# Two filters per product and one 1024-column add in the mixing stage of a spectral convolution

## Chip, cores and metric

The kernel runs on one core of a Trainium2 chip. The metric is the device time of one execution in microseconds. Names of engines: PE is the TensorE matmul unit (PEld its weight load), DVE is VectorE, ACT is ScalarE, POOL is GpSimd, SP is SyncE, which here issues DMAs. All data is 32-bit float.

## What is computed

Two layers run one after the other on a tensor of 4 images, 128 channels, 128 x 128 pixels. The first is a state-space (Mamba) layer over windows of 8 x 8 pixels. The second is a convolution in the frequency domain followed by a small network per pixel. The change lies in the second layer, in the lines that multiply by Phi and Theta (W1, gelu and W2 follow):

```
Xf = jnp.fft.rfft2(z, axes=(-2, -1))
Phi = Phi_f_real + 1j * Phi_f_imag
Uf = Xf[:, :, None, :, :] * jnp.conj(Phi)[None, None]
U = jnp.fft.irfft2(Uf, s=(gx, gy), axes=(-2, -1))
S = jnp.einsum('bdlxy,lhd->bhxy', U, Theta)
...
H = jax.nn.gelu(H, approximate=False)
out = jnp.einsum('bhxy,dh->bdxy', H, W2) + b2[None, :, None, None]
```

There are 16 filters (the index l). For each, Theta[l] mixes 128 channels into 128, and Phi[l] is a complex factor for each frequency. Since both are linear, the kernel does the mixing before the inverse transform: for each frequency row y (65 of them, the half spectrum) it forms the sum over l of conj(Phi[l]) times (Theta[l] times Xf).

## The kernel before

Four stages follow each other: the state-space layer (`mamba_layer`, about two thirds of the time), the forward transform (`spectra`), the mixing (`mix`), and the inverse transform with the network (`images_and_mlp`). Only `mix` is touched. Its instructions stand in the order in which the Python code calls them, on each engine by itself; engines wait for each other through semaphores that the framework sets where tiles are written, read and reused.

`mix` goes over the 65 rows y, and within a row over the 16 filters k. For one row the input is `o.xk`: 128 channels by 4 images (B) by real and imaginary part (r) by 128 frequencies in x. The steps of one filter:

- `products` (lines 657 to 665) has PE multiply: for each r and each image, one product of 128 x 128 with `theta[:, k]`, 128 columns. In 32-bit float each product is two matmul records in the profile, each with its weight load. [...] `products` returns four terms, each a tile, the part r of the result that it goes to, and which of three factor tables (real, imaginary, negated imaginary) it is scaled by.
- `mine` (lines 681 to 690) has DVE take each of the four terms from PSUM, scale it by the factor and add it to the accumulator `acc` of its row: one operation of 512 columns each.
- `ahead` (lines 667 to 679) does the same for the row after, on ACT and POOL: ACT scales the term from PSUM into a tile `part` in SBUF, and POOL adds `part` to `acc` (the first filter is written to `acc` by ACT without an add).

`APART` on line 642 names the filters that go to ACT and POOL: 0, 2, 5, 7, 10 and 12. The other ten go to DVE. While DVE adds its ten filters of row y, ACT and POOL gather their six of row y+1; the accumulator (3 buffers) then passes to DVE, whose first operation of a row therefore depends on POOL's last add for that row. PE does the products of both in the order of the loop on lines 712 to 720; row 0 has no row before it, so there DVE does all 16.

`finish` (lines 692 to 709) writes an accumulator to memory, with 32 DMAs on SP's queue: 2 for image 0, and for the other images 6 with 4 mirrored ones each. It is called for row y-1 in row y after filter 3, and then `load` fetches the input of row y+3 (4 buffers).

Of the kernel before, what the change touches and what calls it, by code (L numbers as in the profile page):

```python
# [13 lines left out]
F32 = mybir.dt.float32  # L14
BF16 = mybir.dt.bfloat16
AF = mybir.ActivationFunctionType
ALU = mybir.AluOpType
PSUM = bass.MemoryType.PSUM

P = 128  # L20
# [8 lines left out]
NL = 16  # L29
# [3 lines left out]
SG = (0, 16, 32, 48, 60, KY)  # L33
# [20 lines left out]

APART = {2: -2, 4: 0, 8: 3, 12: 6, 14: 10, 18: 15, 20: 17, 24: 20}

# [4 lines left out]
HQ = 32  # L61


def mamba_layer(tc, d, x, x1, zb, deltas, dus, results):
# [16 lines left out]
    with ExitStack() as ctx:  # L81
# [91 lines left out]
        def take(slot, f):  # L173
            takes.setdefault(slot, []).append(f)
# [197 lines left out]
        def fetch(s):  # L372

            if 0 <= s < U * R:
                r, k = divmod(s, U)
                u = SimpleNamespace(o=rs[r], r=r, h=k // 16, ch=k // 8 % 2, i=k // 2 % 4, jp=k % 2, apart=k in APART)
                units[s] = u
# [18 lines left out]
        for r in range(R):  # L396
            for k, at in APART.items():
                take(U * r + at - 3, partial(fetch_du, U * r + k))
# [226 lines left out]
def load_row(tc, xf, y, t):  # L625
    for q in range(2):
        tc.nc.sync.dma_start(t[:, :, :, q], xf[y // YG][y % YG, :, :, q])


def mix(tc, theta, phi, sign, xf, firsts, sf, mirrors, first):  # L630

    nc = tc.nc  # L640
    B = len(sf)
    APART = (0, 2, 5, 7, 10, 12)
    with ExitStack() as ctx:
        ctx.enter_context(tc.manual_schedule())
        sb = ctx.enter_context(tc.tile_pool(name="m_sb", bufs=3, reuse_waits="tile"))
        ps = ctx.enter_context(tc.tile_pool(name="m_ps", bufs=4, space=PSUM, reuse_waits="tile"))
        nc.vector.tensor_scalar(phi[0], phi[0], sign, None, ALU.mult)
        nc.vector.tensor_scalar(phi[2], phi[1], -1.0, None, ALU.mult)
        rows = {y: SimpleNamespace(xk=t) for y, t in enumerate(firsts)}

        def load(y):
            if y < KY:
                rows[y] = o = SimpleNamespace()
                o.xk = sb.tile([P, B, 2, 2, W // 2], F32, tag="xk", name="xk", bufs=4)
                load_row(tc, xf, y, o.xk)

        def products(o, k):
            v = []
            for r in range(2):
                t = ps.tile([P, B, P], F32, tag=f"v{r}", name=f"p_v{r}")  # L660
                for b in range(B):
                    nc.tensor.matmul(t[:, b], o.xk[:, b, r], theta[:, k], start=True, stop=True)  # L662
                v.append(t)

            return [(v[of], r, by) for first in range(2) for r, of, by in ((0, first, first), (1, 1 - first, 2 * first))]

        def ahead(y, k):
            if y == KY:
                return
            o = rows[y]  # L670
            if k == APART[0]:
                o.acc = sb.tile([P, B, 2, P], F32, tag="acc", name="acc")
            for i, (v, r, by) in enumerate(products(o, k)):
                into = part = o.acc[:, :, r]
                if k != APART[0] or i >= 2:
                    part = sb.tile([P, B, P], F32, tag="part", name="part", bufs=8)
                nc.scalar.activation(part, v, AF.Copy, scale=phi[by][:, k, y : y + 1])  # L677
                if part is not into:
                    nc.gpsimd.tensor_tensor(into, into, part, ALU.add)  # L679

        def mine(y, k):
            o = rows[y]
            if y + k == 0:
                o.acc = sb.tile([P, B, 2, P], F32, tag="acc", name="acc")
            for i, (v, r, by) in enumerate(products(o, k)):
                into, factor = o.acc[:, :, r], phi[by][:, k, y : y + 1]
                if y + k == 0 and i < 2:
                    nc.vector.tensor_scalar(into, v, factor, None, ALU.mult)
                else:
                    nc.vector.scalar_tensor_tensor(into, v, factor, into, ALU.mult, ALU.add)  # L690

        def finish(y):
            if y >= 0:
                o = rows.pop(y)
                at = y - 1 if 0 < y < KY - 1 else KY - 2 + y // (KY - 1)
                g = int(np.searchsorted(SG, at, "right")) - 1
                for q in range(2):
                    hs = slice(q * (P // 2), (q + 1) * (P // 2))
                    nc.sync.dma_start(sf[0][g][:, q, at - SG[g]], o.acc[:, 0, :, hs])
                if y in [k if k < KY else KY - 1 for k in SG[1:]]:  # L700
                    first(g)
                for b in range(1, B):
                    for r in range(2):
                        part = o.acc[:, b, r].rearrange("p (q h) -> p q h", h=HQ)
                        nc.sync.dma_start(sf[b][:, :, r, at], part)

                        for k in range(4):
                            to, of = (slice(32 * j + (k < 2), 32 * j + 32) for j in (k, k ^ 1))
                            nc.sync.dma_start(mirrors[b][to, :, r, at], part[of])

        load(2)
        for y in range(KY):
            for k in range(NL):
                if k not in APART or y == 0:
                    mine(y, k)
                if k in APART:
                    ahead(y + 1, k)
                if k == 3:
                    finish(y - 1)
                    load(y + 3)  # L720
        finish(KY - 1)


# [118 lines left out]
def conv_kernel(ctx: ExitStack, tc: tile.TileContext, d, out):  # L842
# [16 lines left out]
    with ExitStack() as stages:  # L859
# [43 lines left out]
        def first_image(g):  # L903
            for q in range(2):
                nc.sync.dma_start(spec[q][:, SG[g] : SG[g + 1]], sf[0][g][:, q])

        mix(tc, m.theta, m.phi, m.sign, xf, m.firsts, sf, mirrors, first_image)
    images_and_mlp(tc, c, spec, sp.close, sf, mirrors, x1, out)

# [74 lines left out]
```

## Time and profile before

| | us |
|---|---|
| median of 3 runs | 9695.65 (9645.32 to 9696.60) |
| profiled execution, its own time | 9703.76 |
| its span, first to last instruction | 9702.0 |
| mixing, first product to last DVE operation of L690 | 7060.0 to 8984.5 |

| engine | busy in the whole span | its part in the mixing, instructions | mean ns |
|---|---|---|---|
| PE | 8698.3 (90%) | L662, 16640 | 277 |
| PEld | 4716.0 (49%) | L662, 16640 | 193 |
| DVE | 8582.0 (88%) | L690, 2622 | 743 |
| ACT | 6311.0 (65%) | L677, 1408 and 128 | 688 and 684 |
| POOL | 8053.3 (83%) | L679, 1408 | 1280 |

The shares over the whole span mix four stages with different limits; what a change in `mix` is worth is read from the stretch between 7060 and 8985. Matmuls are pipelined: the 277 ns of one is longer than the distance to the next, so distances are read from counts over a stretch. In a group of the profile, "idle before" is the time in which the engine stood before these instructions, with the engine and line that ended most of it. The granted clock is the share of TensorE's full clock.

### The profile page before, as it was taken

Reading aid. Unit: us, or ns where it says so; the run is one execution under the profiler, and the core shown is the slowest. Engines: PE = TensorE matmul, PEld = TensorE weight load, DVE = VectorE, ACT = ScalarE, POOL = GpSimd, SP = SyncE. Lnnn points to the kernel's source line nnn. Section 1 sums busy time; section 2 is a strip of 40 time slices with the busy share of each in tenths; the row PEclk is TensorE's granted clock in tenths of the full one; section 3 lists DMA queues with packets and bytes.
Section 4 is the critical chain, followed back from the end, with each engine's and each line's share of the span. In section 5 each row is a group of like instructions: output and inputs, shape, how many; then the busy total and the mean of one; then the engine's idle time right before and its main releaser. Section 6 shows DMA issues by size and latency. Waiting matters only on the chain. (4 is left out here: it accounts for less than half of the span.)

```text
span 9702.0 us, 140663 instructions
## 1 busy us (share of the span) xinstructions
PE 8698.3 (90%) x46868; PEld 4716.0 (49%) x46868; DVE 8582.0 (88%) x6989; ACT 6311.0 (65%) x12163; POOL 8053.3 (83%) x3196
## 2 busy tenths in 40 slices
PE   7888888888888888888888888887899999999999
PEld 3333333333333333333333333332899999999665
DVE  6999999999999999999999999998589999999433
ACT  5777777777777777777776777775545555554333
POOL 6999999999999999999999999997389999998120
PEclk8999999999999999999999999998999999999999
DMA  6787777788887787787787777876832323232453
GB/s 180 236 243 236 235 239 236 235 242 237 236 241 233 235 241 231 236 242 237 235 245 230 237 241 237 237 241 191 241 79 52 59 51 58 52 58 52 161 206 130
DMA packets 1504097, 1878.58 MB, mean 194 GB/s; under 512 B 681828, under 2 KB 749684, under 8 KB 1496308
## 3 DMA queue, kind: packets, MB, share of 16 engines
q1 hardware_dynamic: 1502796, 1869.45, 66.3%
q8 instruction: 373, 6.11, 0.3%
q14 instruction: 352, 2.88, 0.1%
q10 hardware_dynamic: 576, 0.14, 0.0%
HBM read 1540.52 MB, written 328.60 MB: 193 GB/s over the span
## 5 line engine op out<-in xcount | busy, mean ns | idle before, releaser
L475 POOL TENSOR_TENSOR hs<-hs,bc 128x2048 f32<-128x2048 f32 x1024 | 4646.9, 4538 | 559.3 <-DVE hs L449 433.0
L449 DVE TENSOR_TENSOR_SCAN hs<-dA,p_du 128x1024 f32<-128x1024 f32 x1536 | 3451.0, 2267 | 0.0
L429 ACT ACTIVATE dA<-dr,A 128x504 f32<-128x504 f32 x3072 | 1996.4, 707 | 9.9 <-DVE hs L449 8.6
L445 DVE TENSOR_TENSOR p_du<-p_du,bc 128x1024 f32<-128x1024 f32 x1536 | 1823.5, 1217 | 174.8 <-PE p_du L414 173.7
L662 PE MATMUL p_v<-theta,xk 128*128 128x128 f32 x16640 | 1881.6, 277 | 46.0 <-ACT part L677 28.1
L690 DVE SCALAR_TENSOR_TENSOR acc<-p_v,phi,acc 128x512 f32<-128x512 f32 x2622 | 1769.7, 743 | 150.3 <-PE p_v L662 124.7
L662 PEld LDWEIGHTS p_v<-theta,xk 128*128 128x128 f32 x16640 | 1876.3, 193 | 51.3 <-ACT part L677 31.9
L679 POOL TENSOR_TENSOR acc<-acc,part 128x512 f32<-128x512 f32 x1408 | 1737.7, 1280 | 140.9 <-ACT part L677 96.0
L414 PE MATMUL p_du<-du,c_rsel 32*128 32x512 f32 x6144 | 1295.6, 655 | 235.8 <-DVE hs L449 232.8
L677 ACT ACTIVATE part<-p_v,phi 128x512 f32<-128x512 f32 x1408 | 884.9, 688 | 547.8 <-PE p_v L662 506.8
L394 POOL TENSOR_TENSOR ur<-ur,bc 128x1024 f32<-128x1024 f32 x512 | 1212.5, 2368 | 16.6 <-DMA ur<-du 16.6
L485 PE MATMUL p_y<-hs,c_ssel 128*32 128x512 f32 x8192 | 1130.1, 624 | 52.4 <-POOL hs L475 52.4
L449 DVE TENSOR_TENSOR_SCAN hs<-p_du,ur 128x1024 f32<-128x1024 f32 x512 | 1165.9, 2277 | 0.0
L242 PE MATMUL p_conv<-tn,W_conv 128*128 128x512 f32 x2016 | 1110.9, 656 | 0.8
L414 PEld LDWEIGHTS p_du<-du,c_rsel 32*128 32x128 f32 x6144 | 358.5, 187 | 896.2 <-issue 525.0
L247 ACT ACTIVATE xc<-p_conv,b_conv 128x512 f32<-128x512 f32 x252 | 173.1, 687 | 884.5 <-PE p_conv L242 884.5
L429 ACT ACTIVATE p_du<-dr,A 128x504 f32<-128x504 f32 x1024 | 701.6, 685 | 33.5 <-DMA dr<-delta 0.2
L208 PE MATMUL ln_back<-ident,cs 128*128 128x128 f32 x2008 | 320.2, 308 | 366.9 <-ACT cs L202 366.9
L242 PEld LDWEIGHTS p_conv<-tn,W_conv 128*128 128x128 f32 x2016 | 340.9, 198 | 528.6 <-issue 310.8
L208 PEld LDWEIGHTS ln_back<-ident,cs 128*128 128x128 f32 x2008 | 268.9, 209 | 586.3 <-ACT cs L202 534.4
L485 PEld LDWEIGHTS p_y<-hs,c_ssel 128*32 128x32 f32 x8192 | 163.1, 109 | 748.2 <-issue 368.9
L257 PE MATMUL p_bc<-xc,c_W_bc 128*128 128x512 f32 x1016 | 498.7, 613 | 0.1
(136 smaller groups left out, 8887.6 us busy)
## 6 DMA issues: line engine op xcount, KB each, us to landing
dr<-delta SPq DMA_DIRECT2D x4096, 256.0 KB
ur<-du SPq DMA_DIRECT2D x1024, 256.0 KB
delta<-dl SPq DMA_DIRECT2D x128, 512.0 KB
du<-du SPq DMA_DIRECT2D x128, 512.0 KB
xf<-x SPq DMA_DIRECT2D x40, 832.0 KB
xk<-xf SPq DMA_DIRECT2D x130, 256.0 KB
xt<-in_x_dram SPq DMA_DIRECT2D x64, 512.0 KB
x<-x1t SPq DMA_DIRECT2D x64, 512.0 KB
```

Source lines behind the costliest of these rows:

```text
L242: nc.tensor.matmul(windows(o.pc), W_conv[:, ch, k], moved, start=(k == 0), stop=(k == K - 1))
L394: nc.gpsimd.tensor_tensor(fetched[s], fetched[s], spread(o.bc[0, h], 2), ALU.mult)
L414: nc.tensor.matmul(u.bank[:, j % 2], c["rsel"][p, u.i], half(u.o.du[p, u.ch], u.h), start=True, stop=True)
L429: nc.scalar.activation(u.dA[:, q, :, 1:], u.delta[:, q].rearrange("p (w t) -> p w t", t=L)[:, :, 1:], AF.Exp, scale=A[:, g : g + 1],)
L445: nc.vector.tensor_tensor(u.bu, u.bu, spread(u.o.bc[0, u.h], 2), ALU.mult)
L449: nc.vector.tensor_tensor_scan(u.hs.rearrange("p q t -> p (q t)"), u.dA.rearrange("p q w t -> p (q w t)"), u.bu.rearrange("p q t -> p (q t)"),
L475: nc.gpsimd.tensor_tensor(hs, hs, spread(u.o.bc[1, u.h], 4), ALU.mult)
L485: nc.tensor.matmul(o.py[h, ch][32 * j : 32 * j + 32], c["ssel"][:, u.i], units[s + j // 2].hs[:, j % 2], start=(u.i == 0), stop=False, ski ...
L662: nc.tensor.matmul(t[:, b], o.xk[:, b, r], theta[:, k], start=True, stop=True)
L677: nc.scalar.activation(part, v, AF.Copy, scale=phi[by][:, k, y : y + 1])
L679: nc.gpsimd.tensor_tensor(into, into, part, ALU.add)
L690: nc.vector.scalar_tensor_tensor(into, v, factor, into, ALU.mult, ALU.add)
```

## The change

Filters are taken in pairs k, k+1. [...] `products` returns four terms, one for each r and each filter of the pair, with the two factors for the real and imaginary result. ACT writes both results of a term into one `part` of 1024 columns (4 buffers in place of 8), and POOL adds it at once. The accumulator's dimensions are reordered to (2, B, 128). The pairs go in a written order, `ORDER`; the pairs that go to ACT and POOL are 0, 6 and 12 (six filters, as before). `finish` and `load` stand behind pair 4.

```diff
-    APART = (0, 2, 5, 7, 10, 12)
+    ORDER = (2, 0, 4, 8, 6, 10, 14, 12)
+    APART = (0, 6, 12)
...
-        ps = ctx.enter_context(tc.tile_pool(name="m_ps", bufs=4, space=PSUM, reuse_waits="tile"))
+        ps = ctx.enter_context(tc.tile_pool(name="m_ps", bufs=2, space=PSUM, reuse_waits="tile"))
...
-                t = ps.tile([P, B, P], F32, tag=f"v{r}", name=f"p_v{r}")
+                t = ps.tile([P, B, 2, P], F32, tag=f"v{r}", name=f"p_v{r}")
                 for b in range(B):
-                    nc.tensor.matmul(t[:, b], o.xk[:, b, r], theta[:, k], start=True, stop=True)
+                    nc.tensor.matmul(t[:, b], o.xk[:, b, r], theta[:, k : k + 2], start=True, stop=True)
                 v.append(t)
-            return [(v[of], r, by) for first in range(2) for r, of, by in ((0, first, first), (1, 1 - first, 2 * first))]
+            return [(v[r][:, :, j], k + j, ((0, 2), (1, 0))[r]) for r in range(2) for j in range(2)]
...
             if k == APART[0]:
-                o.acc = sb.tile([P, B, 2, P], F32, tag="acc", name="acc")
-            for i, (v, r, by) in enumerate(products(o, k)):
-                into = part = o.acc[:, :, r]
-                if k != APART[0] or i >= 2:
-                    part = sb.tile([P, B, P], F32, tag="part", name="part", bufs=8)
-                nc.scalar.activation(part, v, AF.Copy, scale=phi[by][:, k, y : y + 1])
-                if part is not into:
-                    nc.gpsimd.tensor_tensor(into, into, part, ALU.add)
+                o.acc = sb.tile([P, 2, B, P], F32, tag="acc", name="acc")
+            for i, (v, f, by) in enumerate(products(o, k)):
+                part = o.acc
+                if k != APART[0] or i:
+                    part = sb.tile([P, 2, B, P], F32, tag="part", name="part", bufs=4)
+                for r in range(2):
+                    nc.scalar.activation(part[:, r], v, AF.Copy, scale=phi[by[r]][:, f, y : y + 1])
+                if part is not o.acc:
+                    nc.gpsimd.tensor_tensor(o.acc, o.acc, part, ALU.add)
...
-            for i, (v, r, by) in enumerate(products(o, k)):
-                into, factor = o.acc[:, :, r], phi[by][:, k, y : y + 1]
-                if y + k == 0 and i < 2:
-                    nc.vector.tensor_scalar(into, v, factor, None, ALU.mult)
-                else:
-                    nc.vector.scalar_tensor_tensor(into, v, factor, into, ALU.mult, ALU.add)
+            for i, (v, f, by) in enumerate(products(o, k)):
+                for r in range(2):
+                    into, factor = o.acc[:, r], phi[by[r]][:, f, y : y + 1]
+                    if first and i == 0:
+                        nc.vector.tensor_scalar(into, v, factor, None, ALU.mult)
+                    else:
+                        nc.vector.scalar_tensor_tensor(into, v, factor, into, ALU.mult, ALU.add)
...
-            for k in range(NL):
+            for k in ORDER:
                 if k not in APART or y == 0:
                     mine(y, k)
                 if k in APART:
                     ahead(y + 1, k)
-                if k == 3:
+                if k == 4:
                     finish(y - 1)
                     load(y + 3)
```

More of the change, by code (lines that the diff above doesn't have):

```diff
@@ L671, in ahead @@
             if k == APART[0]:
-                o.acc = sb.tile([P, B, 2, P], F32, tag="acc", name="acc")
-            for i, (v, r, by) in enumerate(products(o, k)):
-                into = part = o.acc[:, :, r]
-                if k != APART[0] or i >= 2:
-                    part = sb.tile([P, B, P], F32, tag="part", name="part", bufs=8)
-                nc.scalar.activation(part, v, AF.Copy, scale=phi[by][:, k, y : y + 1])
-                if part is not into:
-                    nc.gpsimd.tensor_tensor(into, into, part, ALU.add)
+                o.acc = sb.tile([P, 2, B, P], F32, tag="acc", name="acc")
[7 more added lines that the diff above has]
+                    nc.gpsimd.tensor_tensor(o.acc, o.acc, part, ALU.add)
         def mine(y, k):
             o = rows[y]
-            if y + k == 0:
-                o.acc = sb.tile([P, B, 2, P], F32, tag="acc", name="acc")
-            for i, (v, r, by) in enumerate(products(o, k)):
-                into, factor = o.acc[:, :, r], phi[by][:, k, y : y + 1]
-                if y + k == 0 and i < 2:
-                    nc.vector.tensor_scalar(into, v, factor, None, ALU.mult)
-                else:
-                    nc.vector.scalar_tensor_tensor(into, v, factor, into, ALU.mult, ALU.add)
+            first = y == 0 and k == ORDER[0]
+            if first:
+                o.acc = sb.tile([P, 2, B, P], F32, tag="acc", name="acc")
+            for i, (v, f, by) in enumerate(products(o, k)):
[5 more added lines that the diff above has]
+                        nc.vector.scalar_tensor_tensor(into, v, factor, into, ALU.mult, ALU.add)
         def finish(y):
@@ L698, in finish @@
                     hs = slice(q * (P // 2), (q + 1) * (P // 2))
-                    nc.sync.dma_start(sf[0][g][:, q, at - SG[g]], o.acc[:, 0, :, hs])
+                    nc.sync.dma_start(sf[0][g][:, q, at - SG[g]], o.acc[:, :, 0, hs])
                 if y in [k if k < KY else KY - 1 for k in SG[1:]]:
@@ L703, in finish @@
                     for r in range(2):
-                        part = o.acc[:, b, r].rearrange("p (q h) -> p q h", h=HQ)
+                        part = o.acc[:, r, b].rearrange("p (q h) -> p q h", h=HQ)
                         nc.sync.dma_start(sf[b][:, :, r, at], part)
```

## The prediction, made before the changed kernel ran

> **What bounds the kernel now.** The page's slices show three parts, and only lines of the mixing function change, so I read the windows of that stage first, then the groups of its lines, then its waits. Columns of the windows: stretch, length, busy time of PE, weight loads, DVE, ACT and POOL with instruction counts, granted clock, DMA.
>
> ```profile
> 7200.00:7400.00 200.00, 196.78 (x1746) 196.40 (x1745) 183.65 (x273) 102.57 (x165) 186.99 (x152) 0.99 0.28 49
> 8600.00:8800.00 200.00, 200.00 (x1792) 199.93 (x1791) 188.96 (x280) 104.55 (x169) 188.68 (x154) 1.00 0.29 52
> ```
>
> PE is full; DVE and POOL are at 94%, ACT at 52%. 1792 matmuls in 200 us are 111.6 ns each. A row has 16 filters x 8 products, and each product is two records (16640 in all for 65 rows), so a row is 256 x 0.1116 = 28.57 us and PE sets it.
>
> ```profile
> L662 PE MATMUL p_v<-theta,xk 128*128 128x128 f32 x16640 | 1881.6, 277 | 46.0 <-ACT part L677 28.1
> L690 DVE SCALAR_TENSOR_TENSOR acc<-p_v,phi,acc 128x512 f32<-128x512 f32 x2622 | 1769.7, 743 | 150.3 <-PE p_v L662 124.7
> L679 POOL TENSOR_TENSOR acc<-acc,part 128x512 f32<-128x512 f32 x1408 | 1737.7, 1280 | 140.9 <-ACT part L677 96.0
> L394 POOL TENSOR_TENSOR ur<-ur,bc 128x1024 f32<-128x1024 f32 x512 | 1212.5, 2368 | 16.6 <-DMA ur<-du 16.6
> ```
>
> DVE waits almost only for PE, never for POOL, though in the built program, before and after, the first DVE instruction of a row carries a wait for POOL: a row's share from POOL must be complete before DVE adds to it. Before, the last POOL filter of a row is 12, and DVE has 13, 14 and 15 (12 operations, 8 us) to do first. From the timeline I take the spacing in a dense stretch (start, length, count):
>
> ```profile
> 7066.69 43.21 DVE L690 SCALAR_TENSOR_TENSOR acc<-p_v,phi,acc 128x512 f32<-128x512 f32 x65 [0.85 <-PE p_v L662]
> 8609.90 25.89 POOL L679 TENSOR_TENSOR acc<-acc,part 128x512 f32<-128x512 f32 x21
> 8619.11 1.84 ACT L677 ACTIVATE part<-p_v,phi 128x512 f32<-128x512 f32 x3 [0.21 <-PE p_v L662]
> 9299.60 1.88 PE L802 MATMUL p_h<-mu,c_W 128*128 128x512 f32 x4
> 9301.32 1.88 PE L811 MATMUL p_o<-g,c_W 128*128 128x512 f32 x4
> ```
>
> DVE: (43.21-0.743)/64 = 0.664 us. POOL: (25.89-1.277)/20 = 1.231, less than the 1.277 of one. ACT: (1.84-0.687)/2 = 0.577, so two are 1.26. A 512-column matmul takes 1.72/4 = 430 ns.
>
> **The change part by part.** The stage runs from 7060.0 to 8984.5, 1924.5 us of the profiled execution's 9703.76.
>
> *Products of 256 columns.* No row here has such a matmul in a stretch: at least half of 430 = 215 ns, at most twice 111.6 = 223. I take 217, the straight line between both rows. A row is then 128 x 0.217 = 27.8 us, 0.8 less than now, at most 50 us over 65 rows. This is the gain if PE stays the bound. A half of a pair (one tile, 8 records) is filled in 1.74 us.
>
> *DVE and ACT* have as many operations as before (40 and 24 a row, 512 columns each). They read PSUM in four runs of 128 instead of one; the same form with four runs on the accumulator runs now at 743 ns, so I add nothing. Bounds: no gain, and 0.3 us each (the strided copy of p_ix, 1.04 us).
>
> *GpSimd* gets 11 adds of 1024 columns for 22 of 512. L394 says 2.37 us. Before, neighbouring adds went to different halves of acc and overlapped by 0.046; now each needs the sum of the one before. I take 2.37 + 0.05 = 2.42; bounds 2.32 (overlap remains) and 2.57 (0.2 for a handoff, as in ACT's 0.21 after PE). A row is 26.6 us, below 28.57, so POOL's total isn't the bound.
>
> *The order of pairs* is the costly part. Call pairs on DVE D and on ACT/POOL A: D2 A0 D4 D8 A6 D10 D14 A12, and A belongs to the next row. A12 now stands last and D2 of the next row first, so the 8 us of cover are gone: DVE stands until POOL has added all four parts of A12. Behind the waiting DVE stand D2's PSUM tile and all products that need DVE's tiles. And PE can't run ahead, because the two buffers of each tile hold two pairs in place of four filters in half the size: slot 0 takes D2, D4, A6, D14; slot 1 A0, D8, D10, A12. PE is in order, so A12 is filled after D10 and D14.
>
> One row from its first DVE operation (T0): D2, D4 and D8 end at 23 x 0.664 + 0.743 = 16.0. This frees the second tile of slot 1; 0.2 later (the 0.21 that PE waited after ACT) PE fills D10's second half, both halves of D14 and the first of A12: 4 x 1.74 = 7.0, so 23.2. To ACT 0.17 (a matmul's 275 ns less its 111.6), two ACT 1.26: 24.6. To POOL 0.06 (a gap in the timeline at 7105.6), four adds 9.68: 34.4, and 0.1 to DVE: the next T0 is at 34.5. Nothing earlier breaks this chain: D4's first half is there at 4.9 (wanted at 5.3), D8's at 9.2 (10.6), D10's at 16.2 (16.0; its 0.2 late is no part of the chain), POOL is through with A6 at 23.5. DVE itself needs 26.6 and stands for 7.6.
>
> *What that does to the clock.* PE ends A0 at 32.4 and can go on with D4 only when DVE has read D2's first tile, 2.9 after T0: 5.1 us idle. Idle gaps of that size are in the state-space stage (last bracket: idle before):
>
> ```profile
> 6642.34 1.13 PE L414 MATMUL p_du<-du,c_rsel 32*128 32x512 f32 x4
> 6652.76 2.08 PE L414 MATMUL p_du<-du,c_rsel 32*128 32x512 f32 x4 [4.05 <-DVE hs L449]
> 6658.35 1.13 PE L414 MATMUL p_du<-du,c_rsel 32*128 32x512 f32 x4
> ```
>
> After 4.05 us the same four matmuls take 2.08 in place of 1.13, until about 5 us later; all gaps over 4 us that I looked at (4.6, 4.7, 6.1, 11.4, 15.4) are followed by 3.5 to 5.6 us of this. So D4's first half takes 3.48, is there at 6.6, and DVE is 1.3 late: 35.7 us a row. The second half ends at 9.2, wanted at 9.25.
>
> [...]
>
> *DMAs.* SP's row of 32 issues takes some 25 us and no new ones are added; finish and load come at the same place behind DVE's last operation, and a longer row gives them more time. The 155 us that ACT waits now for the accumulator's stores go away, off the path.
>
> *Sum.* Row 0 has no such wait at its start: 1.9 to the first tile, 52 DVE operations until D14's first tile is free (34.5), then 0.3 + 1.74 + 0.17 + 1.26 + 0.06 + 9.68 + 0.1 = 13.3; with 2 us of half clock at the start, as now (272 matmuls in 32.4 us instead of 30.4), 52. Then 63 x 35.7 = 2249 and DVE's last row 26.6: 2328, 403 more than 1924.5. On 9703.76 this is 10,107; on the median of the runs, 9695.65, 10,099. I say 10,100.
>
> **The rivals.**
> *PE stays the bound* (faster). If POOL's last add came before DVE is through with D14, the row would be PE's 27.8: -50, 9,646. For it: PE at 100% today and no DVE wait for POOL. It decides from the point where the chain above is 28.57 or less, 5.9 us shorter; all four adds would have to take 0.95 each, against 2.37 in L394. 5%.
> *The wait, with the clock kept up*: 34.5 a row, 52 + 2174 + 27 = 2253, +328, 10,024. For it: gaps of 2.5 and 2.7 us at 6646 and 6690 were followed by 1.13 at first. Against it: the gap here is 5. 20%.
> *The wait with dearer operations*: 0.2 more a POOL add and half clock for 7 us give some 37.2 a row, +500, 10,195; DVE at 0.3 us more each would add 24 x 0.3 = 7 a row and pass 10,500. Against the last: the present accumulator is strided and costs nothing. 10%.
> *A smaller wait* (9,745 to 9,960): PE takes the fills in another way than I see. 4%. *No change* 2%.
>
> **How the numbers follow.** Wait and half clock have 59%, with a time of 10,100. The range: low end from the warm clock with POOL at 2.32 and DVE at 0.655 (34.0 a row, 2220, +296: 9,992) less 47 for the spread of the runs (9645 to 9697); high end from half clock for 7 us (36.9 a row, +478: 10,174) and some 36 of the 54 us that the stage now takes beyond PE's 1857 and the 13 at its end. So 9,945 to 10,210, with about 84% inside: nearly all of the first case and the second rival, half of the third. A change under 0.5% (48 us) can't be told from none here. Faster 4% (the PE rival is -50, just past the bound, with 1 of its 5% inside it), same 3%, slower 93%.
>
> **What would show it.** In the profile after: DVE's first operation of each row idle 7 to 9 us behind POOL's acc, 64 times (some 500 us in all); PE idle about 5 us a row behind DVE, and mean clock in this stage near 0.93; POOL adds at 2.3 to 2.5 us; rows 34 to 37 us apart; PE's 256-column matmuls 215 to 223 ns apart in dense stretches. If DVE waits for PE instead, or POOL's wait is under 2 us, the prediction is wrong. If the wait is there and the clock stays at 1.0, it is the second rival.

## The result: 4.4% slower, and the profile after

| | before | changed |
|---|---|---|
| median us | 9696.12 (9645.32 to 9703.24, 4 runs) | 10115.11 (10089.85 to 10115.90, 4 runs) |
| profiled execution, its own time | 9703.76 | 10115.90 |
| mixing, first product to end of DVE's last | 1924.5 | 2336.2 (7059.8 to 9396.0) |

The ratio is 1.0438, with an interval of 1.0399 to 1.0476. The stage alone is longer by 411.7 us, and the profiled executions differ by 412.1: everything else is as it was.

The groups of the changed kernel that stand for the three shown of before (count, busy time, mean ns, idle time before and its main cause):

```profile
L663 PE MATMUL p_v<-theta,xk 128*128 128x256 f32 x8320 | 1976.9, 401 | 362.5 <-DVE acc L694 346.5
L694 DVE SCALAR_TENSOR_TENSOR acc<-p_v,phi,acc 128x512 f32<-128x512 f32 x2622 | 1743.2, 743 | 587.8 <-POOL acc L681 490.2
L681 POOL TENSOR_TENSOR acc<-acc,part 128x1024 f32<-128x1024 f32 x704 | 1656.7, 2357 | 635.2 <-ACT part L679 595.1
```

All three engines now stand idle: PE 362 us where it had 46, DVE 588 where it had 150, POOL 635 where it had 141. DVE's idle time is put down to POOL, which it did not wait for before. The mean of a DVE operation is still 743 ns.

Two stretches of 200 us (columns as before):

```profile
7200.00:7400.00 200.00, 172.04 (x733) 145.40 (x731) 148.09 (x224) 82.01 (x139) 146.23 (x63) 0.93 0.23 41
8600.00:8800.00 200.00, 169.24 (x712) 142.68 (x712) 145.98 (x220) 81.65 (x138) 148.39 (x64) 0.93 0.23 41
```

PE went from full to 85%, DVE and POOL from 94% to 73%, and the granted clock from 1.0 to 0.93. No engine is the bound; a chain through all four is. The timeline of one row shows it (start, length, idle before):

```profile
8217.40 5.42 PE L663 MATMUL p_v<-theta,xk 128*128 128x256 f32 x24 [0.45 <-DVE acc L694]
...
8224.70 5.36 DVE L694 SCALAR_TENSOR_TENSOR acc<-p_v,phi,acc 128x512 f32<-128x512 f32 x8 [7.44 <-POOL acc L681]
...
8227.57 14.01 PE L663 MATMUL p_v<-theta,xk 128*128 128x256 f32 x56 [4.75 <-DVE acc L694]
...
8231.23 21.16 DVE L694 SCALAR_TENSOR_TENSOR acc<-p_v,phi,acc 128x512 f32<-128x512 f32 x32 [1.17 <-PE p_v L663]
...
8249.24 4.74 ACT L679 ACTIVATE part<-p_v,phi 128x512 f32<-128x512 f32 x8 [6.28 <-PE p_v L663]
8250.65 16.81 POOL L681 TENSOR_TENSOR acc<-acc,part 128x1024 f32<-128x1024 f32 x7 [1.33 <-ACT part L679]
...
8260.33 5.36 DVE L694 SCALAR_TENSOR_TENSOR acc<-p_v,phi,acc 128x512 f32<-128x512 f32 x8 [7.94 <-POOL acc L681]
```

DVE starts a row at 8224.70, after 7.44 us behind POOL. PE had stopped at 8222.8 and goes on 4.75 us later, when DVE has emptied a tile. DVE is through its first pair in 5.36 and then waits 1.17 for the next products. A12 reaches ACT at 8249.24 and POOL at 8250.65; the first four of its seven adds are A12's, and 9.7 us later DVE starts the next row, 35.6 us after the last. Over all rows these starts are 35.8 us apart on average (before: 28.57 us of PE work).

### The profile page after: what moved, and what is told of

Read it like the earlier page. It is cut to its first block, busy times and chain, and to the rows that moved or that the text cites. A ratio compares the mean times of both kernels' runs of the same rounds, so it can differ in the third digit from the quotient of the medians.

```text
span 10113.9 us, 121963 instructions
## 1 busy us (share of the span) xinstructions
PE 8793.8 (87%) x38548; PEld 4505.0 (45%) x38548; DVE 8556.4 (85%) x6989; ACT 6263.9 (62%) x12163; POOL 7974.0 (79%) x2492
## 5 line engine op out<-in xcount | busy, mean ns | idle before, releaser
L663 PE MATMUL p_v<-theta,xk 128*128 128x256 f32 x8320 | 1976.9, 401 | 362.5 <-DVE acc L694 346.5
L694 DVE SCALAR_TENSOR_TENSOR acc<-p_v,phi,acc 128x512 f32<-128x512 f32 x2622 | 1743.2, 743 | 587.8 <-POOL acc L681 490.2
L681 POOL TENSOR_TENSOR acc<-acc,part 128x1024 f32<-128x1024 f32 x704 | 1656.7, 2357 | 635.2 <-ACT part L679 595.1
L663 PEld LDWEIGHTS p_v<-theta,xk 128*128 128x128 f32 x8320 | 1666.1, 202 | 673.1 <-issue 362.3
L679 ACT ACTIVATE part<-p_v,phi 128x512 f32<-128x512 f32 x1408 | 835.7, 705 | 1220.4 <-PE p_v L663 1213.9
```

What stands on the lines that cost most here:

```text
L663: nc.tensor.matmul(t[:, b], o.xk[:, b, r], theta[:, k : k + 2], start=True, stop=True)
L679: nc.scalar.activation(part[:, r], v, AF.Copy, scale=phi[by[r]][:, f, y : y + 1])
L681: nc.gpsimd.tensor_tensor(o.acc, o.acc, part, ALU.add)
```

## The experiments

The order of the pairs, the coarse units, the clock and the wide add are all part of one change. The first four kernels take them apart.

**Another order, nothing else.**

```diff
-    ORDER = (2, 0, 4, 8, 6, 10, 14, 12)
+    ORDER = (0, 2, 6, 4, 8, 12, 10, 14)
```

> The changed kernel with one line altered: the pairs go A0 D2 A6 D4 D8 A12 D10 D14, so that two DVE pairs (16 operations, 10.6 us) follow the last POOL pair of a row. Theory (the row change waits for POOL's sum because A12 stands last): DVE's wait for POOL falls from 490 us to under 30, a row from 35.7 to about 28.7 us, the stage from 2336 to 1885 to 1940 us, the whole to 9,660 to 9,715 us, at or below the kernel before. Rival (the pairs themselves cost: two buffers in place of four, PSUM read in four runs, 1024-column adds): the row stays above 33 us and the whole above 10,000 us.

Measured: 9680.62 us against 9694.30 for the kernel before (ratio 0.9987, 0.9977 to 0.9996). One line gives back the whole loss. DVE's wait for POOL is gone from the list; the stage's waits (engine, who it waited for, us in total, times, longest) are now:

```profile
ACT part L679 <- PE p_v L663: 377.1, 117, 6.2
ACT acc L679 <- DMA mirrors<-acc: 276.7, 34, 15.6
DVE acc L694 <- PE p_v L663: 142.9, 66, 11.3
```

So in this order neither 256-column products nor two buffers nor PSUM read in four runs costs anything near 400 us. In the second line ACT waits for an accumulator whose stores are still under way. The changed kernel has no such wait; the kernel before has it too, but shorter:

```profile
ACT acc L677 <- DMA mirrors<-acc: 155.1, 24, 12.8
```

**The order on single filters.** The kernel before, with its finer tiles, adds and four buffers, in the order of the changed one:

```diff
-    APART = (0, 2, 5, 7, 10, 12)
+    ORDER = (2, 3, 0, 1, 4, 5, 8, 9, 6, 7, 10, 11, 14, 15, 12, 13)
+    APART = (0, 1, 6, 7, 12, 13)
...
-            for k in range(NL):
+            for k in ORDER:
```

> The kernel before, single filters, 128-column products, four buffers, 512-column adds, with only the order of the changed kernel: filters 2 3 0 1 4 5 8 9 6 7 10 11 14 15 12 13, of which 0 1 6 7 12 13 go to ACT and POOL. Theory: the wait belongs to the order, not to the pairs: about 34.8 us a row, DVE idle behind POOL about 7 us a row, whole about 10,040 us. Rival (the coarse tiles cause it): the finer tiles hide the turn, and the time stays within 50 us of 9,696.

Measured, in one run: 9937.02 us, 243 above before. The waits of this kernel hold this line:

```profile
DVE acc L692 <- POOL acc L680: 385.0, 126, 5.9
```

The order alone brings the wait, which settles against the rival, but 100 us less than expected. The 126 waits are two a row: each half of the accumulator has its own last add, and DVE's first operation starts when the first half is ready. I had reckoned with one wait for the whole. So of the 419 us lost, 243 come with the order on single filters too, and the other 176 only where the order meets the coarser units. This run doesn't tell wide tiles from wide adds; narrow adds in the changed kernel, below, give back 108.

This run also shows something of the clock. PE waits 205.8 us for DVE in this kernel, in 69 waits, 3.2 us at the longest, and equal gaps are not all followed by the same clock. Here are the 8 us behind two of them, of 3.21 and 3.22 us:

```profile
8197.08:8205.08 8.00, 8.00 (x71) 8.00 (x72) 8.00 (x13) 0.00 (x0) 5.12 (x5) 1.00 0.21 33
8229.12:8237.12 8.00, 8.00 (x57) 8.00 (x58) 7.70 (x12) 0.00 (x0) 5.10 (x5) 0.79 0.23 35
```

The first stretch has the full clock and 71 matmul records, the second a mean of 0.79 and 57.

**The clock.** The changed kernel with more work for PE: the second tile of pair 0 for ACT is computed three times over, into the same place.

```diff
-                for b in range(B):
+                for b in [*range(B)] * (1 + again * r):
                     nc.tensor.matmul(t[:, b], o.xk[:, b, r], theta[:, k : k + 2], start=True, stop=True)
...
-            for i, (v, f, by) in enumerate(products(o, k)):
+            for i, (v, f, by) in enumerate(products(o, k, 2 * (k == APART[0]))):
```

> The changed kernel with work added: PE makes the second tile of pair 0's products for ACT three times over (16 more matmul records a row, 3.5 us), so that its idle time at the row change falls from 5.0 to about 1.5 us. Theory (after the long gap the next products run at half clock and make DVE 1.3 us late): the clock stays at 1.0, DVE's wait for PE after its first 8 operations goes, a row falls from 35.7 to about 34.6 us, the whole by 70 to 85 us to about 10,035 us, though PE does 6% more. Rival (the half clock is hidden by the wait for POOL, or the clock doesn't follow the gap): 10,115 us or more.

Measured: 10023.81 us, ratio to before 1.0338 (1.0321 to 1.0355); 91 us faster than the changed kernel's 10115.11, with 1024 matmul records more. The group of DVE and a stretch:

```profile
L694 DVE SCALAR_TENSOR_TENSOR acc<-p_v,phi,acc 128x512 f32<-128x512 f32 x2622 | 1738.2, 743 | 505.9 <-POOL acc L681 485.0 <-PE p_v L663 20.8
```

```profile
7200.00:7400.00 200.00, 185.56 (x837) 157.09 (x837) 153.11 (x232) 81.09 (x136) 151.62 (x65) 1.00 0.24 43
```

The clock is back at 1.00, and DVE's idle time behind PE is 20.8 us where the waits of the changed kernel have 96.7:

```profile
DVE acc L694 <- PE p_v L663: 96.7, 101, 3.9
```

The wait for POOL is nearly as long as in the changed kernel, 485 us against 490. The half clock was thus a cost of its own on top of the wait: 91 us in all, 1.4 a row, of which 76 are DVE's wait for PE.

**Narrow adds.** The changed kernel with two adds of 512 columns, each right behind its ACT operation:

```diff
                 for r in range(2):
                     nc.scalar.activation(part[:, r], v, AF.Copy, scale=phi[by[r]][:, f, y : y + 1])
-                if part is not o.acc:
-                    nc.gpsimd.tensor_tensor(o.acc, o.acc, part, ALU.add)
+                    if part is not o.acc:
+                        nc.gpsimd.tensor_tensor(o.acc[:, r], o.acc[:, r], part[:, r], ALU.add)
```

> The changed kernel with each 1024-column add of POOL split into two of 512, one for each half of the accumulator, each behind its own ACT operation. Theory: POOL takes 1.23 us an add and 27.1 us a row against 26.6, but the chain at the row change shortens: the first add starts 0.6 us earlier, and DVE's first operation needs only the half that is ready 1.2 us before the last. About 1.0 us less a row, 65 us in all, 10,050 us. Rival (the larger add saves POOL fixed cost where it counts): 10,115 us or more.

Measured: 10006.68 us (1.0325, 1.0309 to 1.0340), 108 us faster than with the wide add, though POOL is busy longer (1734 us against 1657). The sign was right and the size, 65 us, too small. DVE's waits show both parts:

```profile
L694 DVE SCALAR_TENSOR_TENSOR acc<-p_v,phi,acc 128x512 f32<-128x512 f32 x2622 | 1755.1, 744 | 474.2 <-POOL acc L681 403.7 <-PE p_v L663 66.5
```

The wait for POOL fell by 87 us (490.2 to 403.7), 1.35 a row where I had 1.0, and the wait for PE, which I had left out, by 30 (96.7 to 66.5). One row of it:

```profile
8207.73 0.75 DVE L694 SCALAR_TENSOR_TENSOR acc<-p_v,phi,acc 128x512 f32<-128x512 f32 x1 [5.83 <-POOL acc L681]
8208.95 4.70 DVE L694 SCALAR_TENSOR_TENSOR acc<-p_v,phi,acc 128x512 f32<-128x512 f32 x7 [0.47 <-POOL acc L681]
...
8211.16 24.55 PE L663 MATMUL p_v<-theta,xk 128*128 128x256 f32 x104 [3.70 <-DVE acc L694]
...
8213.81 2.73 DVE L694 SCALAR_TENSOR_TENSOR acc<-p_v,phi,acc 128x512 f32<-128x512 f32 x4 [0.16 <-PE p_v L663]
```

DVE starts on the first half while POOL adds the second. PE's gap shrinks to 3.70 us, and in this row DVE is only 0.16 late after its first pair, against 1.17 in the changed kernel's.

**One pair later.** The changed kernel with A12 one place earlier:

```diff
-    ORDER = (2, 0, 4, 8, 6, 10, 14, 12)
+    ORDER = (2, 0, 4, 8, 6, 10, 12, 14)
```

> The changed kernel with the last two pairs exchanged: D10 A12 D14, so that one DVE pair (8 operations, 5.3 us) follows the last POOL pair. Theory: part of the cover is back, DVE's wait for POOL falls from 7.7 to about 5 us a row, but D14 now waits 1.8 us for PE, because A12 is filled before it: a row about 34.9 us, 60 us less in all, about 10,055 us. Rival (any DVE pair behind A12 hides its sum): 9,750 us or less.

Measured, in one run: 10014.74 us, 100 us less than the changed kernel where I expected 60. One row:

```profile
8207.99 5.36 DVE L694 SCALAR_TENSOR_TENSOR acc<-p_v,phi,acc 128x512 f32<-128x512 f32 x8 [4.54 <-POOL acc L681]
...
8210.86 13.74 PE L663 MATMUL p_v<-theta,xk 128*128 128x256 f32 x56 [4.17 <-DVE acc L694]
...
8214.28 15.89 DVE L694 SCALAR_TENSOR_TENSOR acc<-p_v,phi,acc 128x512 f32<-128x512 f32 x24 [0.93 <-PE p_v L663]
...
8232.24 5.36 DVE L694 SCALAR_TENSOR_TENSOR acc<-p_v,phi,acc 128x512 f32<-128x512 f32 x8 [2.06 <-PE p_v L663]
```

DVE waits 4.54 us for POOL (expected: about 5), 0.93 after its first pair, and 2.06 before D14 (expected: 1.8). So one DVE pair behind the last POOL pair is indeed not cover enough. PE's gap is 4.17 us here.

**Four accumulators.** What was left in the first experiment is the wait for the stores, so the better order and the kernel before each got a fourth buffer, in both lines that allocate it. In the kernel with pairs:

```diff
-                o.acc = sb.tile([P, 2, B, P], F32, tag="acc", name="acc")
+                o.acc = sb.tile([P, 2, B, P], F32, tag="acc", name="acc", bufs=4)
```

> The first experiment (A0 D2 A6 D4 D8 A12 D10 D14) with a fourth accumulator buffer, so that ACT no longer waits for the accumulator's stores (277 us in all there). Theory: PE's idle time in the stage falls from 71 to about 30 us, a row to 28.7 us, the stage to about 1886 us, the whole to 9,645 to 9,675 us, some 30 us below the first experiment. Rival (those waits are ACT's own slack): no change from 9,681.

> The kernel before with a fourth accumulator buffer and nothing else. Theory: it too loses time to the accumulator's stores, and comes to PE's bound, 28.6 us a row, about 1875 us for the stage, the whole to 9,640 to 9,660 us; then the pairs with the better order win nothing over single filters, since what 256 columns save on PE (0.5 us a row) goes into the wait for coarser tiles. Rival (products of 256 columns are worth their 0.5 to 0.8 us a row): this one stays 30 us or more above the run with pairs and four buffers.

Measured: 9648.12 with pairs (0.9949, 0.9936 to 0.9961), 32 us below the first experiment, and 9648.93 with single filters (0.9954, 0.9941 to 0.9968). Waiting for one of only three accumulators had cost the kernel before some 47 us, and the two come out alike, as expected. PE's group with single filters, which had 46.0 us of idle time with three buffers:

```profile
L662 PE MATMUL p_v<-theta,xk 128*128 128x128 f32 x16609 | 1857.3, 275 | 3.7 <-DVE acc L690 2.7 <-ACT part L677 0.8
```

A stretch of the pairs, then one of the single filters:

```profile
8000.00:8200.00 200.00, 196.85 (x900) 169.34 (x898) 186.21 (x282) 99.96 (x170) 182.50 (x78) 1.00 0.32 62
```

```profile
8000.00:8200.00 200.00, 200.00 (x1794) 200.00 (x1793) 188.77 (x281) 106.16 (x169) 190.35 (x155) 1.00 0.32 62
```

Single filters fill PE. With pairs PE loses time each row. The timeline shows the start of two rows of PE work, 28.49 us apart. 128 matmuls at 215.3 ns, the spacing in the last experiment, are 27.56 us, so 0.9 us a row is lost; 0.45 of it is a wait for a tile that DVE empties:

```profile
8200.56 28.04 PE L663 MATMUL p_v<-theta,xk 128*128 128x256 f32 x128 [0.45 <-DVE acc L694]
...
8229.05 6.28 PE L663 MATMUL p_v<-theta,xk 128*128 128x256 f32 x28 [0.45 <-DVE acc L694]
```

**Half pairs, alternating.** Against the kernel with pairs and four accumulators, the unit that goes to an engine is one tile (one r of a pair), four tiles in one ring (`bufs=4` for one tag). The units go in the order of their numbers, with `finish` and `load` behind unit 5:

```diff
-    ORDER = (0, 2, 6, 4, 8, 12, 10, 14)
-    APART = (0, 6, 12)
+    APART = (0, 2, 5, 8, 11, 13)
...
-        def products(o, k):
-            v = []
-            for r in range(2):
-                t = ps.tile([P, B, 2, P], F32, tag=f"v{r}", name=f"p_v{r}")
+        def products(o, u):
+            k, r = u // 2 * 2, u % 2
+            t = ps.tile([P, B, 2, P], F32, tag="v", name="p_v")
...
+            return [(t[:, :, j], k + j, ((0, 2), (1, 0))[r]) for j in range(2)]
```

> Products of 256 columns and adds of 1024 as in the changed kernel, four accumulator buffers, but the unit that is handed to DVE or to ACT and POOL is one tile (one r of a pair, 4 DVE operations), four tiles in one ring, and the 16 units of a row alternate: units 0, 2, 5, 8, 11 and 13 go to ACT and POOL, two units of DVE follow the last. Theory: what the pairs with the better order lose is PE's wait for a tile that DVE or ACT empties too late (a row is 28.5 us there, PE's work 27.9); handing out finer units removes it, a row comes to 27.9 us, the stage to about 1831 us, the whole to 9,600 to 9,615 us, below both kernels. Rival (another bound, DVE or POOL, sits just under 28.5 us): no better than 9,648.

Measured: 9588.89 us against 9696.95 for the kernel before (0.9890, 0.9873 to 0.9906), faster than both kernels, and below what I expected:

```profile
8000.00:8200.00 200.00, 200.00 (x929) 176.47 (x928) 192.24 (x291) 104.73 (x174) 187.92 (x81) 1.00 0.30 53
```

PE is full again, now with 929 matmuls of 256 columns: 215.3 ns each, 27.6 us a row. Unit, ring and order changed together here, so the run doesn't say what each is worth.

## Why the prediction was right, point by point

- *The 256-column matmul.* Taken at 217 ns, between 215 and 223 (the straight line through both rows gives 217.7); with PE full it takes 215.3 to 215.5, half of the 512-column one. A row saves 1.0 us where I had 0.8. The changed kernel doesn't collect it; the last experiment does.
- *DVE and ACT at no extra cost.* DVE 743 ns before and after; right. One ACT operation takes 705 ns in place of 688, but eight in a row take 4.74 us, so they follow each other at (4.74-0.687)/7 = 0.579 where I had 0.577.
- *The wide add* at 2.42 with its dependence: 2.357 alone, and four adds of a pair take 9.68 to 9.70 where the timeline has them by themselves, as in the sum.
- *The wait for POOL* at 7.6 us a row: 490.2 us in 64 times, 7.66. That it belongs to the place of A12 is shown by the first and second experiment, and with one pair of cover by the fifth.
- *The gap of PE* at 5.1 us (its own terms, 34.5 + 2.9 - 32.4, give 5.0): 4.75 and 5.24 in two rows. *The half clock behind it*, making DVE 1.3 us late: in 63 rows of the timeline DVE was late after its first pair, by 0.78 to 1.30 us, by 1.30 in 30 of them, 1.16 on average. The third experiment shows that the clock does it: at 1.00, DVE's idle time behind PE is 20.8 us against 96.7. All 63 gaps of PE at these row changes (4.73 to 5.52 us) were followed by a mean granted clock of 0.50 to 0.59 over the next 3.4 us.
- *Why all 63* were followed by it was not shown. In the kernel before, all 15 gaps of PE over 4 us behind its first instruction (4.05 to 15.38 us) were followed by a mean clock of 0.50 over the next 1 us. So the rows that I went by held, but they set no limit of 4 us: the same listing has a gap of 2.18 us, at 6664.67, followed by 2.04 in place of 1.13 (mean clock 0.52), which the second rival left out. Nor does the length alone decide: a longer gap, 2.67 us at 6646.14, was followed by 1.13 at a clock of 1.00, and in the second experiment gaps of 3.21 and 3.22 us were followed by a mean clock of 1.00 and 0.79 over 8 us. In the records of the granted clock of the two profiled runs, before and changed, it is 1.0 or 0.5 and changes only at whole multiples of 3.413 us from one another (121 and 229 changes); no run shows what sets it.
- *The sum.* 2328 us for the stage, measured 2336.2: row 0 took 52.9 us (52), the other rows 35.82 (35.7). The whole was 10,115 against 10,100. That it comes so close is in part luck: DVE's lateness was smaller than the 1.3 us a row of the sum, and the rest of the row, 35.82 - 1.16 = 34.66, longer than its 34.5.
- *The rivals.* PE as the bound fell: PE is at 85%. The wait with the clock kept up is what the third experiment built: 10,024, as the rival's 10,024, with rows 34.39 us apart in its timeline against 34.5. The wait with dearer operations fell with the durations above.
- *The waits for the stores*, which I called off the path in the kernel before: with a fourth buffer it gained 47 us, so part of them was on the path. In the changed kernel they do vanish behind the longer row. The sum went by the whole stage and isn't touched by this, but the reason was wrong.

## What to carry to other kernels

Where a helper engine prepares an accumulator that another takes over, compare the work that the taker has after the helper's last piece is handed out with the helper's chain, both in microseconds. The helper's total load didn't show it here: POOL's fell from 94% to 73% while DVE's wait for it went from nothing to 7.7 us a row. Doubling the unit (two filters, one wide add) saves PE 1.0 us a row, but POOL's last chain of four adds doubles (4 x 1.23 to 4 x 2.42 us), and tiles come free in pieces twice as large. So order and unit have to be chosen together: here the same wide products lost 4.4% in one order of pairs and won 1.1% in alternating half units with one more accumulator buffer, which alone is worth 0.5% on single filters. A stall of some 5 us on PE cost more than its length here, since the work behind it started at half clock (a mean of 0.50 to 0.59 over the first 3.4 us; with the clock kept at 1.00 the third experiment was 91 us faster).

## What the runs showed that I had not expected

- The clock falls to half after shorter gaps than the 4 us that I went by, and not after every gap of one length: a mean of 0.52 followed 2.18 us in the kernel before, and in the second experiment 1.00 followed 3.21 us and 0.79 followed 3.22.
- More matmuls made the kernel faster, as I expected once I had seen the gap, and by more than expected: 1024 records added to fill it took 91 us off, where I had 70 to 85.
- A POOL stage that is busier by 78 us in sum (narrow adds) is faster by 108 us, where I had 65: the first half is handed over early, and PE's gap falls from about 5 to 3.7 us.
- The three accumulator buffers of the kernel before cost it 47 us, though ACT, which waits for them, is busy only 52% of the time. PE's idle time behind ACT was 28.1 us there and is 0.8 us with the fourth.
